# PSUM shared differently in a fused attention and mixture-of-experts kernel: three single banks for the maxima's scores, four for the exponentials', maxima read by head

## The chip, the cores and the metric

One core of one Trainium2 chip. The metric is device time in microseconds of one execution of the whole program. All arithmetic is in f32.

## What is computed

A transformer layer in "sandwich" form on x of shape (8, 1024, 256): layer norm, causal attention with 16 heads of 16, a second layer norm and a residual; then layer norm, a mixture of 8 experts (the best two of each token), layer norm and residual. The part that matters here is the attention:

```python
score = einsum('bhnd,bhmd->bhnm', q, k) * scale
score = where(causal, score, -inf)
attn = softmax(score, axis=-1)
out = einsum('bhnm,bhmd->bhnd', attn, v)
```

The experts come after it: `gu = flat @ gate_up[e] + bias`, a clipped gated product, `down`, and the two chosen results weighted and added.

## The kernel before

**Units and slots.** The attention works in 32 units: a unit is one batch entry (8) and a group of four heads (4 groups). For every unit two things are done, one unit apart. First the *maxima*: scores with the query on the partitions, of which only the row maxima are kept (`maxima_tiles`, L649). Then, one unit later, the *exponentials* of the same scores with the key on the partitions and the row maximum folded into the product (`values_tiles`, L758), so that ACT can take the exponential straight from PSUM (L796) and TensorE (PE) can multiply the result with the values (`weighted`, L810, matmuls at L825). So the main loop (L1151) in round u does the maxima of unit u and the exponentials of unit u - 1. Round 0 has maxima only, the last round exponentials only.

A unit has nine steps (`STEPS`, L635): two EDGE, three TWO, four WHOLE. In an EDGE step a 128x512 tile of scores ends on the diagonal; in a WHOLE step it lies under it; a TWO step packs two shorter tiles of one head into 512 columns. Every step is done for two pairs of heads, so a unit has 18 *slots*, and the attention 576, of which 558 have both halves. A slot (L1180 to L1232) issues in this order:

1. PE: four score matmuls, for the maxima's two heads (`sa`, L693) and for the exponentials' two heads (`sb`, L788). The four heads lie on different quarters of the partitions; a TWO step takes twice four, by part. Each matmul shows as two records in the trace.
2. ACT: the two exponentials (L796).
3. DVE, and ACT in TWO steps: the reading of `sa` (`reduce`, L698). WHOLE: one reduction of both heads (L709). EDGE: for each head an addition of the causal mask with a running maximum (L703, and the reading of its accumulator). TWO: a reduction of the blocks that need no mask for both heads (L718 or L724) and then a copy by ACT of the diagonal blocks of both heads into SBUF (L728), which POOL masks (L742) and DVE reduces (L747) later.
4. PE: one half of the weighted sums of an earlier step (L825), then background.

**Background.** Layer norms, projections, transposes, the output projection, routing: generators that yield pieces with a cost on each engine. `pump` (L1105) spends them against a credit that each slot earns (L1198 to L1204, with fixed numbers such as 1.22 us of DVE for a WHOLE slot). The order of PE, DVE, ACT and SP is the order of the source (`manual_schedule`, L1139), and POOL's is held by `in_order`.

**PSUM.** A bank is a tile of 128x512 f32, and the pools hold eight. During attention: `ps_a`, two buffers of two banks, a buffer for the maxima's scores of one slot (`sa`); `ps_v`, one bank for the weighted sums; `ps_b`, three single banks that rotate among the exponentials' scores (two a slot) and all of the background. In the last round pair 1 of the exponentials' scores takes a buffer of `ps_a` (L774). In the experts: `ps_gu`, four banks for the gate and up products of a quarter (L1305, read by DVE at L1317 and L1321), `ps_x`, one bank, and `ps_b`, three, for the down product (L1336) and what is left of the background. A bank is written again only when the reading of its last tile is over: PE waits at the first matmul of the new tile.

Of the kernel before, what the change touches and what calls it, by code (L numbers as in the profile page):

```python
# [11 lines left out]
F32 = mybir.dt.float32  # L12
AF = mybir.ActivationFunctionType
ALU = mybir.AluOpType
AX = mybir.AxisListType
PSUM = bass.MemoryType.PSUM

P = 128
# [40 lines left out]
def attn_moe_kernel(  # L59
# [15 lines left out]
    nc = tc.nc  # L75
    B, S, D = x.shape
# [3 lines left out]
    HG = P // HS  # L80
    NG = H // HG
# [3 lines left out]
    QC = 512  # L85
# [41 lines left out]
    cmask = const.tile([P, QC], F32, name="cmask")  # L127
    nc.gpsimd.memset(cmask, 0.0)
    nc.gpsimd.affine_select(
        out=cmask[:, QC - P :], in_=cmask[:, QC - P :], compare_op=ALU.is_ge, fill=NEG,  # L130
# [6 lines left out]
        out=lower, in_=lower, compare_op=ALU.is_gt, fill=0.0,  # L137
# [5 lines left out]
        out=upper, in_=upper, compare_op=ALU.is_gt, fill=0.0,  # L143
# [6 lines left out]
        out=before, in_=before, compare_op=ALU.is_gt, fill=0.0,  # L150
# [252 lines left out]
    tp = ctx.enter_context(tc.tile_pool(name="tables", bufs=1))  # L403
    ap2 = ctx.enter_context(tc.tile_pool(name="attn2", bufs=2))

    ps_b = ctx.enter_context(tc.tile_pool(name="ps_b", bufs=3, space=PSUM))

    with ExitStack() as attn:

# [1 line left out]
        ap1 = attn.enter_context(tc.tile_pool(name="attn1", bufs=1))  # L411
        ap3 = attn.enter_context(tc.tile_pool(name="attn3", bufs=2))
        ptp = attn.enter_context(tc.tile_pool(name="pt", bufs=3))
        ps_a = attn.enter_context(tc.tile_pool(name="ps_a", bufs=2, space=PSUM))
        ps_v = attn.enter_context(tc.tile_pool(name="ps_v", bufs=1, space=PSUM))


# [231 lines left out]
        def maxima_tiles(u):  # L649

            b, g = divmod(u, NG)
            qP, kP = qPs[u % NU], kPs[u % NU]
            mx = mxs[u % 2]
            edges = {}

            def rows(c):
                yield piece(dve=0.2)
                nm = ap2.tile([P, HG, n], F32, tag="nm", name=f"nm_{u}_{c}")
                nc.vector.tensor_reduce(nm, mx[:, :, ts(c, n), :], AX.X, ALU.max, negate=True)
                yield piece(pe=0.15, act=0.3, after=1)  # L660
                ps = ps_b.tile([HG * n, P], F32, tag="b", name=f"nmps_{u}_{c}")
                nc.tensor.transpose(ps, nm.rearrange("p h i -> p (h i)"), ident)
                nmT = ap2.tile([HG * n, P], F32, tag="nmT", name=f"nmT_{u}_{c}")
                nc.scalar.copy(nmT, ps)
                for hh in range(HG):
                    nc.sync.dma_start(
                        out=qP[hh * HS + DH : hh * HS + DH + 1, ts(c, QC)].rearrange(
                            "o (i q) -> o i q", q=P
                        ),
                        in_=nmT[ts(hh, n), :],  # L670
                    )

            left = [
                sum(c in {i // n for i, _, _ in tiles} for _, tiles, _ in STEPS)
                for c in range(NC)
            ]

            def of_two(k):

                (i, _, w), (i2, _, _) = STEPS[k][1]  # L680
                return slice(i, i2 + 1, i2 - i), w == P

            def pair_of_heads(k, pair):
                kind, tiles, _ = STEPS[k]
                ps = ps_a.tile([P, 2, QC], F32, tag="a", name=f"sa_{u}_{k}_{pair}")

                def scores(hh, part):
                    if part == len(tiles):
                        return
                    i, c, w = tiles[part]  # L690
                    at = sum(t[2] for t in tiles[:part])
                    r = ds((2 * pair + hh) * HS, HS)
                    nc.tensor.matmul(  # L693
                        ps[:, hh, ds(at, w)], lhsT=qP[r, ts(i, P)], rhs=kP[r, ds(c * QC, w)],
                        start=True, stop=True,
                    )

                def reduce():  # L698
                    heads = ts(pair, 2)
                    i, c, w = tiles[0]  # L700
                    if kind == EDGE:
                        for hh in range(2):
                            nc.vector.tensor_tensor_reduce(  # L703
                                out=ps[:, hh, :], in0=ps[:, hh, :], in1=cmask,
                                scale=1.0, scalar=NEG, op0=ALU.add, op1=ALU.max,
                                accum_out=mx[:, 2 * pair + hh, i, 0:1],
                            )
                    elif kind == WHOLE:
                        nc.vector.tensor_reduce(mx[:, heads, i, 2:3], ps, AX.X, ALU.max)  # L709
                    else:  # L710
                        both, short = of_two(k)
                        if k not in edges:
                            edges[k] = ap2.tile(
                                [P, HG, 2, P], F32, tag="edge", name=f"edge_{u}_{k}"
                            )
                        blocks = ps.rearrange("p h (b k) -> p h b k", k=P)
                        if short:
                            nc.vector.tensor_reduce(  # L718
                                mx[:, heads, tiles[1][0], 0:1], ps[:, :, P : 3 * P],
                                AX.X, ALU.max,  # L720
                            )
                            at = blocks[:, :, 0:4:3, :]
                        else:
                            nc.vector.tensor_reduce(  # L724
                                mx[:, heads, both, 0], blocks[:, :, 0:4:2, :], AX.X, ALU.max
                            )
                            at = blocks[:, :, 1:4:2, :]
                        nc.scalar.copy(edges[k][:, heads], at)  # L728

                return scores, reduce  # L730

            def counted_off(k):
                for c in {i // n for i, _, _ in STEPS[k][1]}:
                    left[c] -= 1
                    if not left[c]:
                        rows_of[u, c] = start(urgent, rows(c))

            def masked_edges(k):

                d = edges.pop(k)  # L740
                yield piece(pool=1.25)
                in_order(nc.gpsimd.affine_select(  # L742
                    out=d, in_=d, compare_op=ALU.is_ge, fill=NEG,
                    base=0, pattern=[[0, HG], [0, 2], [-1, P]], channel_multiplier=1,
                ))
                yield piece(dve=1.2, after=1)
                nc.vector.tensor_reduce(mx[:, :, of_two(k)[0], 1], d, AX.X, ALU.max)  # L747
                counted_off(k)

            def done(k):  # L750
                if k in edges:
                    start(urgent, masked_edges(k))
                else:
                    counted_off(k)

            return pair_of_heads, done

        def values_tiles(u):  # L758
# [11 lines left out]
            def pair_of_heads(k, pair):  # L770
                if k not in state:
                    state[k] = ptp.tile([P, HG, QC], F32, tag="pT", name=f"pT_{u}_{k}")
                pT = state[k]
                if u == B * NG - 1 and pair:  # L774
                    both = ps_a.tile([P, 2, QC], F32, tag="a", name=f"sb_{u}_{k}_{pair}")
                    banks = [both[:, hh, :] for hh in range(2)]
                else:
                    banks = [
                        ps_b.tile([P, QC], F32, tag="b", name=f"sb_{u}_{k}_{2 * pair + hh}")
                        for hh in range(2)  # L780
                    ]

                def scores(hh, part):
                    if part == len(STEPS[k][2]):
                        return
                    c, j, off, at = list(parts(k))[part]
                    r = ds((2 * pair + hh) * HS, HS)
                    nc.tensor.matmul(  # L788
                        banks[hh][:, ds(at, QC - off)], lhsT=kP[r, ts(j, P)],
                        rhs=qP[r, ds(c * QC + off, QC - off)],  # L790
                        start=True, stop=True,
                    )

                def exps():
                    for hh in range(2):
                        nc.scalar.activation(pT[:, 2 * pair + hh, :], banks[hh], AF.Exp)  # L796

                return scores, exps
# [446 lines left out]
    def pool(name, bufs, **where):  # L1245
        return ctx.enter_context(
            tc.tile_pool(name=name, bufs=bufs, reuse_waits="tile", **where)
        )
# [2 lines left out]
    m4 = pool("moe4", 4)  # L1251
    m2 = pool("moe2", 2)
    m1 = pool("moe1", 1)
    ps_gu = pool("ps_gu", 4, space=PSUM)
    ps_x = pool("ps_x", 1, space=PSUM)

    def load_tile(i):
# [298 lines left out]
```

## Time and profile before

| | |
|---|---|
| runs (3) | median 2213.28 us, 2211.36 to 2213.5 |
| the profiled execution | 2208.65 us, its span 2206.9 us |
| granted clock of TensorE | 0.992 of full speed |
| attention, both halves | from about 60 to 1372 us |
| last round, exponentials only | about 1374 to 1405 us |
| experts | from about 1407 us, the last layer norm ends the span |
| idle time of PE in the span | 64 us |
| DVE busy in 60 to 1400 us | 996 us |
| ACT busy in 60 to 1400 us | 839 us |

The profile is a hardware trace of one execution. PE stands for matmuls, PEld for the loading of their stationary operand, DVE, ACT, POOL and SP for the vector, scalar, GpSimd and sync engines. A line of a group has: line, engine, operation, what it writes and reads with shapes, how many; then busy us and mean ns of one; then the idle time of the engine just before them and what ended most of it. A line of the timeline has: start (us), length (us), engine, line, operation, tiles, shapes, how many merged; in brackets the idle time before and what ended it. A line of the stretches has for each engine its busy time and its count, then the granted clock, the share of DMA and GB/s.

### The profile page before, as it was taken

How to read it: one execution, taken by the hardware profiler on the slowest of the kernel's cores; microseconds unless marked ns; L12 is line 12 of the kernel's file. 1: busy time of each engine (PE TensorE's matmuls, PEld its weight loads, DVE VectorE, ACT ScalarE, POOL GpSimd, SP SyncE). 2: the span in 40 equal slices, each digit the busy share in tenths (PEclk: the TensorE clock that was granted, in tenths of full speed). 3: DMA queues.
4: the chain of work that ended last, by engine and by line, in shares of the span. 5: the costliest groups of instructions: out<-in, count | busy, mean ns of one | idle time of the engine just before them, and what ended most of it. 6: DMA issues, size and time to landing. Idle time of an engine off the chain costs nothing. (4 is left out here: it accounts for less than half of the span.)

```text
span 2206.9 us, 44890 instructions
## 1 busy us (share of the span) xinstructions
PE 2143.1 (97%) x16697; PEld 1330.8 (60%) x16697; DVE 1633.1 (74%) x3738; ACT 1086.1 (49%) x2169; POOL 1055.7 (48%) x1217
## 2 busy tenths in 40 slices
PE   7999999999999999999999999989999999999995
PEld 4444544544445445445444544678888888888885
DVE  4775777867767776786786787586667888888776
ACT  3666665665666666666666666431212322233222
POOL 3421652563573472482483364455444544445443
PEclk9999999999999999999999999999999999999998
DMA  4001102102101111111110111557657777877773
GB/s 107 17 10 34 29 12 59 41 21 59 33 29 38 50 33 26 45 50 22 50 50 13 39 43 38 173 198 252 220 203 260 261 269 259 273 260 243 261 268 123
DMA packets 138739, 246.70 MB, mean 112 GB/s; under 512 B 17472, under 2 KB 101592, under 8 KB 136600
## 3 DMA queue, kind: packets, MB, share of 16 engines
q1 hardware_dynamic: 124536, 208.22, 30.4%
q0 software_dynamic: 12768, 35.01, 4.2%
q8 instruction: 133, 2.18, 0.4%
q14 instruction: 86, 0.70, 0.1%
q10 hardware_dynamic: 1216, 0.58, 0.1%
HBM read 171.79 MB, written 55.23 MB: 103 GB/s over the span
## 5 line engine op out<-in xcount | busy, mean ns | idle before, releaser
L796 ACT ACTIVATE pT<-sb 128x512 f32<-128x512 f32 x1152 | 625.0, 595 | 409.4 <-PE sb L788 380.4
L788 PE MATMUL sb<-qP,kP 32*128 32x512 f32 (+3 forms) x3072 | 712.9, 524 | 2.9 <-DMA qP<-nmT 1.8
L693 PE MATMUL sa<-kP,qP 32*128 32x512 f32 (+3 forms) x3072 | 655.4, 525 | 3.4 <-DVE mx L703 1.4
L1308 PE MATMUL gu<-xsT,wg 128*128 128x256 f32 x2208 | 501.7, 379 | 0.8 <-ACT xsT L1290 0.7
L1308 PEld LDWEIGHTS gu<-xsT,wg 128*128 128x128 f32 x2208 | 418.4, 190 | 58.2 <-ACT xsT L1290 1.4
L805 POOL TENSOR_SCALAR_AFFINE_SELECT pT<-pT 128x512 f32<-128x512 f32 x256 | 159.6, 639 | 596.7 <-ACT pT L796 591.4
L709 DVE TENSOR_REDUCE mx<-sa 128x2 f32<-128x1024 f32 x256 | 311.5, 1218 | 112.3 <-PE sb L788 108.7
L1319 ACT ACTIVATE sig<-gate 128x256 f32<-128x256 f32 x276 | 114.9, 416 | 546.6 <-DVE gate L1317 545.3
L825 PE MATMUL av<-pT,vpad 128*32 128x256 f32 (+1 forms) x5120 | 345.6, 367 | 1.1 <-DVE avs L836 0.9
L693 PEld LDWEIGHTS sa<-kP,qP 32*128 32x128 f32 x3072 | 228.9, 185 | 189.0 <-issue 98.2
L1324 POOL TENSOR_TENSOR sig<-sig,gate 128x256 f32<-128x256 f32 x276 | 204.2, 742 | 268.8 <-ACT sig L1319 266.9
L788 PEld LDWEIGHTS sb<-qP,kP 32*128 32x128 f32 x3072 | 299.4, 184 | 41.4 <-ACT pT L796 7.2
L825 PEld LDWEIGHTS av<-pT,vpad 128*32 128x32 f32 x5120 | 116.4, 108 | 287.6 <-issue 210.2
L1339 PE MATMUL dn<-wd,act 128*128 128x256 f32 x1104 | 265.6, 381 | 7.8 <-DVE act L1329 7.4
L1317 DVE TENSOR_SCALAR gate<-gu,bs 128x256 f32<-128x256 f32 x276 | 131.8, 478 | 151.0 <-PE gu L1308 136.5
L1339 PEld LDWEIGHTS dn<-wd,act 128*128 128x128 f32 x1104 | 202.8, 190 | 39.4 <-DVE act L1329 15.4
L703 DVE CUSTOM_DVE_ANT_0 sa<-sa,cmask 128x512 f32<-128x512 f32 x256 | 178.0, 697 | 52.8 <-PE sb L788 28.3
L1349 POOL DMA_INDIRECT ytd<-ys,places x138 | 138.9, 1007 | 132.1 <-DVE ys L1345 104.6
L1046 POOL DMA_INDIRECT xsd<-xn,slots x128 | 126.8, 991 | 47.1 <-issue 29.6
L718 DVE TENSOR_REDUCE mx<-sa 128x2 f32<-128x512 f32 x128 | 88.1, 688 | 75.5 <-PE sb L788 49.7
L1329 DVE SCALAR_TENSOR_TENSOR act<-up,sig 128x256 f32<-128x256 f32 x276 | 128.3, 465 | 14.3 <-POOL sig L1324 14.3
L1321 DVE TENSOR_SCALAR up<-gu,bs 128x256 f32<-128x256 f32 x276 | 130.7, 473 | 0.0
(204 smaller groups left out, 2390.8 us busy)
## 6 DMA issues: line engine op xcount, KB each, us to landing
wg<-_L_ffn_gate_up_proj_dram SPq DMA_DIRECT2D x69, 1024.0 KB
wd<-in_L_ffn_down_proj_dram SPq DMA_DIRECT2D x69, 512.0 KB
xs<-xsd SPq DMA_DIRECT2D x65, 258.0 KB
yy<-ytd SPq DMA_DIRECT2D x15, 1024.0 KB
bs<-biasd SPq DMA_DIRECT2D x69, 132.0 KB
x<-in_L_attn_x_dram SPq DMA_DIRECT2D x16, 512.0 KB
x1d<-y SPq DMA_DIRECT2D x16, 512.0 KB
x<-x1d SPq DMA_DIRECT2D x16, 512.0 KB
```

Of the source, the lines that this page charges most:

```text
L693: nc.tensor.matmul(ps[:, hh, ds(at, w)], lhsT=qP[r, ts(i, P)], rhs=kP[r, ds(c * QC, w)], start=True, stop=True,)
L703: nc.vector.tensor_tensor_reduce(out=ps[:, hh, :], in0=ps[:, hh, :], in1=cmask, scale=1.0, scalar=NEG, op0=ALU.add, op1=ALU.max, accum_out ...
L709: nc.vector.tensor_reduce(mx[:, heads, i, 2:3], ps, AX.X, ALU.max)
L788: nc.tensor.matmul(banks[hh][:, ds(at, QC - off)], lhsT=kP[r, ts(j, P)], rhs=qP[r, ds(c * QC + off, QC - off)], start=True, stop=True,)
L796: nc.scalar.activation(pT[:, 2 * pair + hh, :], banks[hh], AF.Exp)
L805: in_order(nc.gpsimd.affine_select(out=d, in_=d, compare_op=ALU.is_ge, fill=0.0, base=0, pattern=[[0, HG], [1, P]], channel_multiplier=-1,))
L825: nc.tensor.matmul(av[ds(hh * HS, HS), ds(off + a - at, z - a)], lhsT=vp[:, j, ds((g * HG + hh) * VS, HS)], rhs=pT[:, hh, a:z],  start=c n ...
L1308: nc.tensor.matmul(ps[:, half, :], lhsT=wg[:, kt, ds(half * FF + f * P, P)], rhs=xT[:, kt, :], start=(kt == 0), stop=(kt == KT - 1),)
L1317: nc.vector.tensor_scalar(gt, ps[:, 0, :], bs[:, f : f + 1], LIMIT, ALU.add, ALU.min)
L1324: in_order(nc.gpsimd.tensor_tensor(sg, sg, gt, ALU.mult))
L1339: nc.tensor.matmul(ps[:, n, :], lhsT=act[:, f, ts(n, P)], rhs=wd[:, f, :], start=(f == 0), stop=(f == FT - 1),)
L1349: put = nc.gpsimd.indirect_dma_start(out=yt_dram[:, :], out_offset=bass.IndirectOffsetOnAxis(ap=places[:, i, n : n + 1], axis=0), in_=y[:, ...
```

## The change

The two pools of attention are cut differently: `ps_a` has three buffers of one bank, `ps_b` four. The maxima's scores are one tile for each head instead of one for a pair. `reduce` works by head: in WHOLE and TWO steps the reductions of a pair become two of half the length, and so does ACT's copy in TWO steps; EDGE already worked by head. In the last round pair 1 of the exponentials takes two single banks of `ps_a`. In the experts `ps_b` stays at four, and `ps_gu` goes from four to three. The costs that the planner uses are left as they were.

```diff
-    ps_b = ctx.enter_context(tc.tile_pool(name="ps_b", bufs=3, space=PSUM))
+    ps_b = ctx.enter_context(tc.tile_pool(name="ps_b", bufs=4, space=PSUM))
...
-        ps_a = attn.enter_context(tc.tile_pool(name="ps_a", bufs=2, space=PSUM))
+        ps_a = attn.enter_context(tc.tile_pool(name="ps_a", bufs=3, space=PSUM))
...
-                ps = ps_a.tile([P, 2, QC], F32, tag="a", name=f"sa_{u}_{k}_{pair}")
+                pss = [
+                    ps_a.tile([P, QC], F32, tag="a", name=f"sa_{u}_{k}_{2 * pair + hh}")
+                    for hh in range(2)
+                ]
...
-                        ps[:, hh, ds(at, w)], lhsT=qP[r, ts(i, P)], rhs=kP[r, ds(c * QC, w)],
+                        pss[hh][:, ds(at, w)], lhsT=qP[r, ts(i, P)], rhs=kP[r, ds(c * QC, w)],
...
-                    heads = ts(pair, 2)
+
                     i, c, w = tiles[0]
-                    if kind == EDGE:
-                        for hh in range(2):
+                    for hh, ps in enumerate(pss):
+                        h = 2 * pair + hh
+                        if kind == EDGE:
                             nc.vector.tensor_tensor_reduce(
-                                out=ps[:, hh, :], in0=ps[:, hh, :], in1=cmask,
+                                out=ps, in0=ps, in1=cmask,
                                 scale=1.0, scalar=NEG, op0=ALU.add, op1=ALU.max,
-                                accum_out=mx[:, 2 * pair + hh, i, 0:1],
+                                accum_out=mx[:, h, i, 0:1],
                             )
-                    elif kind == WHOLE:
-                        nc.vector.tensor_reduce(mx[:, heads, i, 2:3], ps, AX.X, ALU.max)
+                        elif kind == WHOLE:
+                            nc.vector.tensor_reduce(mx[:, h, i, 2:3], ps, AX.X, ALU.max)
...
+                            if short:
+                                nc.vector.tensor_reduce(
+                                    mx[:, h, tiles[1][0], 0:1], ps[:, P : 3 * P], AX.X, ALU.max
+                                )
+                                at = blocks[:, 0:4:3, :]
+                            else:
+                                nc.vector.tensor_reduce(
+                                    mx[:, h, both, 0], blocks[:, 0:4:2, :], AX.X, ALU.max
+                                )
+                                at = blocks[:, 1:4:2, :]
+                            nc.scalar.copy(edges[k][:, h], at)
...
-                if u == B * NG - 1 and pair:
-                    both = ps_a.tile([P, 2, QC], F32, tag="a", name=f"sb_{u}_{k}_{pair}")
-                    banks = [both[:, hh, :] for hh in range(2)]
-                else:
-                    banks = [
-                        ps_b.tile([P, QC], F32, tag="b", name=f"sb_{u}_{k}_{2 * pair + hh}")
-                        for hh in range(2)
-                    ]
+                at, tag = (ps_a, "a") if u == B * NG - 1 and pair else (ps_b, "b")
+                banks = [
+                    at.tile([P, QC], F32, tag=tag, name=f"sb_{u}_{k}_{2 * pair + hh}")
+                    for hh in range(2)
+                ]
...
-    ps_gu = pool("ps_gu", 4, space=PSUM)
+    ps_gu = pool("ps_gu", 3, space=PSUM)
```

## The prediction

> **What bounds the kernel now.** I read the page's shares first, then the groups, the stretches, and last the timeline of single slots.
>
> ```profile
> PE 2143.1 (97%) x16697; PEld 1330.8 (60%) x16697; DVE 1633.1 (74%) x3738; ACT 1086.1 (49%) x2169; POOL 1055.7 (48%) x1217
> ...
> L796 ACT ACTIVATE pT<-sb 128x512 f32<-128x512 f32 x1152 | 625.0, 595 | 409.4 <-PE sb L788 380.4
> L788 PE MATMUL sb<-qP,kP 32*128 32x512 f32 (+3 forms) x3072 | 712.9, 524 | 2.9 <-DMA qP<-nmT 1.8
> ...
> L709 DVE TENSOR_REDUCE mx<-sa 128x2 f32<-128x1024 f32 x256 | 311.5, 1218 | 112.3 <-PE sb L788 108.7
> ```
>
> ```profile
> 60.00:1400.00 1340.00, 1328.61 (x12752) 641.45 (x12749) 996.11 (x2144) 839.13 (x1621) 649.74 (x722) 1.00 0.14 36
> ```
>
> TensorE (PE) sets the pace; ACT and DVE mostly wait for it. The second fence is attention's steady stretch (PE, PEld, DVE, ACT, POOL busy): PE 1328.6 of 1340 us, DVE 996, ACT 839. That hides PE's waits, because a matmul's end is modelled. They show in starts. Call S the start of a slot's four score matmuls and R the start of what PE does next. With nothing waiting, R - S is 1.07 us (median 1.071 in the 369 one-tile slots). The tail, R to the next S, is fixed too: 0.569 us for one half of weighted sums alone, more with background.
>
> A WHOLE slot:
>
> ```profile
> 731.92 0.70 PE L788 MATMUL sb<-qP,kP 32*128 32x512 f32 x2
> ...
> 732.98 0.64 PE L825 MATMUL av<-pT,vpad 128*32 128x256 f32 x8
> 733.09 1.23 DVE L709 TENSOR_REDUCE mx<-sa 128x2 f32<-128x1024 f32 x1 [0.85 <-PE sb L788]
> 733.13 1.08 ACT L796 ACTIVATE pT<-sb 128x512 f32<-128x512 f32 x2 [0.99 <-PE sb L788]
> 733.55 0.19 PEld L693 LDWEIGHTS sa<-kP,qP 32*128 32x128 f32 x2 [0.41 <-issue]
> ...
> 733.56 0.91 PE L788 MATMUL sb<-qP,kP 32*128 32x512 f32 x2
> ```
>
> The row at 733.56 lasts 0.91 where 731.92 has 0.70: its second matmul waited 0.21 us for a ps_b bank, until the first exponential ended at 733.72 (release to PE 0.06). R comes at 734.83 instead of 734.62. Such waits, slot by slot over the 552 readable slots, are 69.2 us. 10.6 of them, in eight slots of the first interior TWO step, belong to the landing of nmT rows; 58.6 us are banks.
>
> A TWO slot:
>
> ```profile
> 703.24 0.64 PE L825 MATMUL av<-pT,vpad 128*32 128x256 f32 x8
> ...
> 703.41 0.68 DVE L724 TENSOR_REDUCE mx<-sa 128x4 f32<-128x512 f32 x1
> 703.45 1.09 ACT L796 ACTIVATE pT<-sb 128x512 f32<-128x512 f32 x2 [0.57 <-PE sb L788]
> ...
> 703.81 0.66 PE L856 MATMUL avt<-ident,avs 128*128 128x128 f32 x4
> 704.40 0.19 PEld L693 LDWEIGHTS sa<-kP,qP 32*128 32x128 f32 x2 [0.17 <-issue]
> ...
> 704.42 0.59 ACT L728 COPY edge<-sa 128x512 f32<-128x512 f32 x1
> ```
>
> R is 703.24, the next S 704.40. The edge copy stands behind both exponentials on ACT and starts at 704.42, after PE is already in the next slot. Today nobody waits: that slot has the other pair of banks.
>
> **The change, part by part.**
>
> *Fourth ps_b bank.* In a slot without background the bank of the second exponential's scores was last used two slots before, not one; with one background tile it is freed by the first exponential, at R + 0.72, while the tail is then 1.15. So the 58.6 us go. The last round, exponentials alone, has eight readable groups with 3.7 us of the same wait: take -3.
>
> *Three single ps_a banks.* Head 0 of a slot needs what head 1 had two slots before, head 1 what head 0 had one slot before. This is the new wait, at the head of PE's queue: behind it stand both sb matmuls, weighted sums and background, and for those wait ACT's exponentials and POOL's masks. It is paid in full unless the tail covers it. When head 0's bank comes free after R:
>
> - WHOLE: DVE starts at R + 0.105 (median of 193 starts from idle), a 512 reduction lasts 0.69 (L718's row, 688 ns for 512), release 0.06: 0.855.
> - EDGE: 0.105 + 0.75 (L703's 697 with its accumulator read, overlapped) + 0.06: 0.915.
> - TWO: exponentials start at R + 0.15, last 1.08, the copy overlaps them by 0.10, takes 0.38 (128x256 from PSUM: L447's rows, 383 ns), release 0.06: 1.57.
>
> Against the tails after these slots (slots, sum of what the tail leaves uncovered):
>
> | tail, us | TWO | EDGE | WHOLE |
> |---|---|---|---|
> | under 0.65 | 24: 24.0 | 37: 12.7 | 69: 19.7 |
> | 0.65-0.9 | 7: 5.1 | 23: 3.1 | 8: 0.9 |
> | 0.9-1.1 | 22: 12.5 | 13: 0 | 71: 0 |
> | 1.1-1.25 | 57: 23.3 | 27: 0 | 33: 0 |
> | 1.25-1.57 | 18: 4.4 | 14: 0 | 0 |
> | above | 55: 0 | 8: 0 | 66: 0 |
> | sum | 69.3 | 15.8 | 20.6 |
>
> 106 us if DVE always starts at once. It does not: with DVE and ACT where they really were in the trace, the sums are 66.4, 41.8 and 44.7, together 153 (short-tailed EDGE slots 0.86 us each, DVE being still at edge reductions of 1.2 us). The lower end could drop by 10: a wait of head 1 lets head 0's reduction start that much earlier relative to R, so in runs of WHOLE slots 0.29 alternates with nothing. A backlog also melts while PE waits, but not wholly, since DVE gets more to do. I take the middle, 130 (TWO 69, EDGE 30, WHOLE 31); ends 96 and 153.
>
> *Reductions by head.* 448 more DVE instructions (256 WHOLE, 192 TWO). Back to back, L709 takes 1138 ns from start to start and L718 601, so the fixed part is 64 ns: 29 us of DVE beside PE's work, inside the choice of 130. Here a rule speaks against the change: the Trainium skill's "Perfetto Trace Analysis", section Optimizing Scalar/DVE Operations, puts the overhead of each DVE operation on PSUM at about 125 ns of engine time and advises grouping where the engine is saturated. By that it is 56 us; the 27 more, spread over 558 slots, make DVE 0.05 us later in each, and in some 200 slots that wait for it add 10 us: +80 in all instead of +70. I use the row; DVE is not saturated in this stretch.
>
> *Edge copies by head.* 192 more on ACT: 192 x (2 x 0.38 - 0.59) = 33 us, beside PE (ACT 839 of 1340); their place on the path is in TWO's 1.57. If ACT had no slack it would cost those 33.
>
> *Nothing moved.* The planner's costs and the score order are unchanged; the built programs keep background in the same slots, and SP issues the same DMAs in the same order.
>
> *Round 0* (maxima alone) is held by DVE part of the time, 50 to 61 us, back-to-back L709: eight reductions split, 0.5 us; with EDGE and TWO take +1 (0 to 3).
>
> *Experts: ps_gu 3, ps_b 4.* A quarter's bank is read by two DVE operations, 478 and 473 ns, while the next two quarters fill; L1308 idles 0.8 us in 2208 matmuls. Zero, from -1 (dn's fourth bank) to +5 if DVE falls two quarters behind near 1406-1550, where background still runs.
>
> **Sum.** +130 - 58.6 - 3 + 1 = +69.4. On the profiled execution, 2208.65 (span 2206.9 and 1.75 around it): 2278. The median of the runs shown stands 4.6 above it: 2283.
>
> In the WHOLE slot above the exchange is small: head 1 would wait till 733.09 + 0.69 + 0.06 = 733.84, 0.28 late, where 0.21 was lost already. In the TWO slot it is not: copy 704.42 to 704.80, PE at 704.86, 0.46 us lost where nothing was.
>
> **Rivals.**
>
> *Backlog melts.* Waits 96: 96 - 58.6 - 2 = +35, 2249. For it: DVE has a quarter of the stretch free. Against: short-tailed EDGE slots are late by background DVE work, which stays. 20%.
>
> *DVE becomes the limit in EDGE and WHOLE.* Waits at 153, and 10 to 20 for the added instructions: some +106, 2319. For it: 0.86 us in short EDGE slots. If, too, the fourth bank did not release the exponentials' scores (the change not doing what it says), 58.6 more; the row at 733.56, ended by an exponential, speaks against that. 17%.
>
> *Faster.* The copy of head 0 gets ahead in TWO: ACT starts the exponentials early enough that the bank is free near R + 1.1, which the 1.1-1.25 tails cover (TWO about 25), and EDGE and WHOLE cost about 10. Then +35 - 60.6: 2188. It decides once all new waits sum below 60. Against: TWO alone gives 69, and its terms, exponentials first and then a copy, are measured rows. 6%.
>
> **How the numbers follow.** Likeliest, the middle: 57%, its own range 2262 to 2305. Range 2243 to 2325: it takes in most of the first rival and half of the second. About 0.2% is what a measurement here can tell from no change. Faster 6%; within it 2%, between the faster and the melting case; slower 92%.
>
> **What would show it.** In the new profile sb's waits on pT should vanish (R - S without the 0.21), while sa's second head waits: for the ACT edge copy after TWO slots, some 0.4 us each, 70 in all, and for DVE mx after EDGE and WHOLE, 60 in all. DVE busy should rise by about 30 us or less where spans overlap less, ACT by about 33, expert stretches unchanged. I am wrong if the waits after TWO are under 40 us, if sb still waits for exponentials, or if DVE's lag grows from slot to slot.

## The result, and the profile after

| | before | after |
|---|---|---|
| runs (4 each) | median 2212.32 us, 2206.56 to 2213.5 | median 2274.7 us, 2272.48 to 2278.0 |
| ratio to before | 1 | 1.0295 (95%: 1.0279 to 1.0311) |
| the profiled execution, its span | 2208.65, 2206.9 us | 2276.76, 2275.0 us |

The change costs 3%. The predicted 2283 us is 8.3 us above the median, and the range held it. The sum behind it was less right than its total: one term fell short by 21 us and others were too high by about as much.

The page of the profile after, its shares and groups:

```profile
PE 2204.6 (97%) x16697; PEld 1359.8 (60%) x16697; DVE 1655.0 (73%) x4186; ACT 1094.3 (48%) x2361; POOL 1058.2 (47%) x1217
...
L796 ACT ACTIVATE pT<-sb 128x512 f32<-128x512 f32 x1152 | 624.3, 595 | 488.6 <-PE sb L788 482.9
L696 PE MATMUL sa<-kP,qP 32*128 32x512 f32 (+3 forms) x3072 | 774.9, 529 | 20.1 <-ACT edge L731 13.4
L788 PE MATMUL sb<-qP,kP 32*128 32x512 f32 (+3 forms) x3072 | 653.5, 525 | 0.4 <-DMA qP<-nmT 0.4
...
L713 DVE TENSOR_REDUCE mx<-sa 128x1 f32<-128x512 f32 x512 | 328.0, 682 | 122.1 <-PE sb L788 103.4
```

Against the page of before: the busy time of sb's matmuls has fallen from 712.9 to 653.5 us, and sa's now has a releaser that was not there, ACT's edge copy (line 731, 728 before). A matmul's modelled end takes a wait of its own operands into its busy time, so most of the 59 us that left L788 must be bank waits. ACT's idle time before the exponentials rose by 79 us: ACT is not the engine that got longer, it waits for a PE that waits.

The stretch of attention, PE, PEld, DVE, ACT, POOL:

```profile
60.00:1400.00 1340.00, 1324.42 (x12096) 637.66 (x12094) 979.10 (x2459) 804.53 (x1716) 624.04 (x690) 0.99 0.13 34
```

PE is as "busy" as before (1328.6), but did 12096 matmul records in the same time where it did 12752, 5% fewer. The count tells what the busy time hides.

A WHOLE slot of after, with the short tail of 0.57 us:

```profile
602.21 0.64 PE L825 MATMUL av<-pT,vpad 128*32 128x256 f32 x8
602.30 1.29 DVE L713 TENSOR_REDUCE mx<-sa 128x1 f32<-128x512 f32 x2 [0.78 <-PE sb L788]
602.38 1.09 ACT L796 ACTIVATE pT<-sb 128x512 f32<-128x512 f32 x2 [0.99 <-PE sb L788]
...
602.78 0.95 PE L696 MATMUL sa<-kP,qP 32*128 32x512 f32 x2
603.05 0.19 PEld L788 LDWEIGHTS sb<-qP,kP 32*128 32x128 f32 x2
603.05 0.70 PE L788 MATMUL sb<-qP,kP 32*128 32x512 f32 x2
...
604.11 0.16 PEld L825 LDWEIGHTS av<-pT,vpad 128*32 128x32 f32 x8 [0.76 <-issue]
```

R is 602.21, the next S 602.78. sa's row lasts 0.95 where an unwaited one has 0.70: its second matmul waited for the bank that DVE's first reduction gave back near 603.0. sb follows at 603.05 with an unwaited 0.70. R - S is 604.11 - 602.78 = 1.33, so 0.26 us is lost; the prediction had 0.28 for this shape.

A TWO slot of after:

```profile
751.59 0.64 PE L825 MATMUL av<-pT,vpad 128*32 128x256 f32 x8
751.72 1.08 ACT L796 ACTIVATE pT<-sb 128x512 f32<-128x512 f32 x2 [0.98 <-PE sb L788]
...
752.41 1.40 PE L696 MATMUL sa<-kP,qP 32*128 32x512 f32 x3
...
752.69 0.66 ACT L731 COPY edge<-sa 128x256 f32<-128x256 f32 x2
...
753.12 0.18 PEld L696 LDWEIGHTS sa<-kP,qP 32*128 32x128 f32 x1 [0.42 <-ACT edge L731]
753.13 0.70 PE L788 MATMUL sb<-qP,kP 32*128 32x512 f32 x2
...
754.19 1.99 PE L600 MATMUL pjq<-xnT,wqT 128*128 128x512 f32 x4
```

R is 751.59, S 752.41. The copy of head 0 starts at 752.69, after both exponentials, and the load of sa's second head at 753.12 names it. Everything behind it on PE's queue is late with it: R - S is 754.19 - 752.41 = 1.78, 0.71 more than unwaited.

**Where the 68.1 us of the span are**, by the starts of PE's work in both traces:

| part | before to after, us | predicted |
|---|---|---|
| round 0, to the first sb (59.7, now 73.4) | +13.7 | +1 |
| round 1 (18 slots) | +8.5 | in the next row |
| slots from 36 on: score groups | +60.1 | +71.4 (130 - 58.6) |
| the same slots: tails | -11.6 | 0 |
| last round, exponentials alone | -2.7 | -3 |
| experts | +0.1 | 0 |

### The profile page after: what moved, and what is told of

It reads as the page before. It is cut to its first block, busy times and chain, and to the rows that moved or that the text cites. A ratio compares the mean times of both kernels' runs of the same rounds, so it can differ in the third digit from the quotient of the medians.

```text
span 2275.0 us, 45369 instructions
## 1 busy us (share of the span) xinstructions
PE 2204.6 (97%) x16697; PEld 1359.8 (60%) x16697; DVE 1655.0 (73%) x4186; ACT 1094.3 (48%) x2361; POOL 1058.2 (47%) x1217
## 5 line engine op out<-in xcount | busy, mean ns | idle before, releaser
L696 PE MATMUL sa<-kP,qP 32*128 32x512 f32 (+3 forms) x3072 | 774.9, 529 | 20.1 <-ACT edge L731 13.4
L788 PE MATMUL sb<-qP,kP 32*128 32x512 f32 (+3 forms) x3072 | 653.5, 525 | 0.4 <-DMA qP<-nmT 0.4
L696 PEld LDWEIGHTS sa<-kP,qP 32*128 32x128 f32 x3072 | 300.0, 186 | 258.2 <-issue 87.7
L713 DVE TENSOR_REDUCE mx<-sa 128x1 f32<-128x512 f32 x512 | 328.0, 682 | 122.1 <-PE sb L788 103.4
L788 PEld LDWEIGHTS sb<-qP,kP 32*128 32x128 f32 x3072 | 251.1, 185 | 19.9 <-issue 1.7
L707 DVE CUSTOM_DVE_ANT_0 sa<-sa,cmask 128x512 f32<-128x512 f32 x256 | 172.6, 711 | 62.8 <-PE sa L696 25.8
L722 DVE TENSOR_REDUCE mx<-sa 128x1 f32<-128x256 f32 x256 | 96.8, 419 | 101.8 <-PE sb L788 54.1
```

The source lines that it names most:

```text
L696: nc.tensor.matmul(pss[hh][:, ds(at, w)], lhsT=qP[r, ts(i, P)], rhs=kP[r, ds(c * QC, w)], start=True, stop=True,)
L707: nc.vector.tensor_tensor_reduce(out=ps, in0=ps, in1=cmask, scale=1.0, scalar=NEG, op0=ALU.add, op1=ALU.max, accum_out=mx[:, h, i, 0:1],)
L713: nc.vector.tensor_reduce(mx[:, h, i, 2:3], ps, AX.X, ALU.max)
L788: nc.tensor.matmul(banks[hh][:, ds(at, QC - off)], lhsT=kP[r, ts(j, P)], rhs=qP[r, ds(c * QC + off, QC - off)], start=True, stop=True,)
```

## The experiments

Ratios are against the kernel before on the same chip; "slot waits" are R - S - 1.07 us summed over the slots after 100 us, as in the prediction: 67.5 before (sb 64.3) and 129.3 after (sa 126.4, sb 2.9). After was not timed again beside the experiments: before stood at 2212.32 us in its measurement and at 2205.5 to 2209.1 in these. A distance to after is therefore good to some us only, and where it matters the one by ratios stands beside the one by medians.

**Is it the splitting or the banks?** Maxima by head, but with the banks shared as before:

```diff
-        ps_a = attn.enter_context(tc.tile_pool(name="ps_a", bufs=3, space=PSUM))
+        ps_a = attn.enter_context(tc.tile_pool(name="ps_a", bufs=4, space=PSUM))
```

(ps_b 3 and ps_gu 4 again.)

> The changed kernel with its reductions and edge copies by head, but with four single banks for the maxima's scores (as many as before), three for ps_b and four for ps_gu: only the splitting is left. Theory (the loss is head 0's bank coming free too late, one slot back): sa has its old distance of two slots, so within 0.5% of before, 2201 to 2224 us; DVE about 25 us busier, ACT up to 33. Rival (the added DVE and ACT instructions are what costs): about the changed kernel's 2275.

2206.55 us, ratio 0.9997 (0.9986 to 1.0008); slot waits 70.1, sb's as before. The 448 reductions and 192 copies more (DVE busy +13.1 us) cost nothing that shows. One bank moved from the maxima to the exponentials costs the rest.

**Does the fourth ps_b bank give anything?** The change with it taken away again, so that one bank lies unused:

```diff
-    ps_b = ctx.enter_context(tc.tile_pool(name="ps_b", bufs=4, space=PSUM))
+    ps_b = ctx.enter_context(tc.tile_pool(name="ps_b", bufs=3, space=PSUM))
```

> The changed kernel with ps_b back at three banks (one bank unused): the loss without the gain. Theory: the waits of sa stay (about 125 us in the steady stretch) and those of sb for exponentials come back where they are not covered by the wait of sa in the same slot: 2300 to 2340 us, 25 to 65 above the changed kernel. Rival (the fourth bank gave nothing, since exponentials limit sb by their own speed): the changed kernel's 2275 within 0.3%.

2300.15 us, 1.042 (1.0393 to 1.0447): 25 us above after (28 by ratios). sb's waits are back at 34.7, while sa's fell to 108.8: while PE waits for the one, the other comes free. So the bank is worth less than the waits that it removes, and the fourth ps_a bank, which is missing, costs more than it gives. Both halves of the exchange are real.

**Is it the copy's place behind the exponentials?** In TWO steps ACT does exponential, copy, exponential, copy:

```diff
...
-                        for _, use in reversed(heads):
-                            use()
+                        if first and second and STEPS[k][0] == TWO:
+                            for hh in range(2):
+                                for _, use in reversed(heads):
+                                    use((hh,))
+                        else:
+                            for _, use in reversed(heads):
+                                use()
```

(`reduce` and the exponentials also take the heads that they work on.)

> The changed kernel with ACT's order in TWO slots turned from exponential, exponential, copy, copy into exponential, copy, exponential, copy. Theory: head 0's bank then comes free near R + 1.09 us instead of 1.57, so the 76 us of waits after TWO slots fall to about 17, the rest stays: 2210 to 2230 us. Rival (it is the copy's length and DVE's reduction that hold the bank, not the place behind the exponentials): over 2260.

2257.72 us, 1.023 (1.0204 to 1.0256): 17 us better than after (14 by ratios, 22 between the profiled executions), not the 45 or more expected. Its waits, in the view of waits (engine, what waited, for whom; us, times, longest):

```profile
PEld sa L696 <- DVE mx L714: 51.7, 134, 1.6
PEld sa L696 <- ACT edge L732: 29.8, 74, 1.5
PEld sa L696 <- DVE mx L708: 28.1, 47, 2.1
```

The same three rows of after:

```profile
PEld sa L696 <- DVE mx L713: 43.6, 112, 1.8
PEld sa L696 <- ACT edge L731: 43.2, 96, 1.5
PEld sa L696 <- DVE mx L707: 17.6, 41, 1.7
```

ACT's row shrinks and both of DVE's grow. Slot by slot: after TWO slots the waits fall from 76 to 41.7 (sa 31.2, sb 10.5), after EDGE they rise from 22.4 to 32.4, after WHOLE from 28.0 to 36.9. The place behind the exponentials was indeed what held the bank: the first copy ends at R + 1.06 in the median of the TWO slots, where after had 1.52. Two things were left out of the expected gain. In 34 of 183 TWO slots the copy still ends after R + 1.15; in 28 of these it stood idle for DVE's reduction of the same scores, and the second exponential stood behind it:

```profile
648.80 0.60 ACT L797 ACTIVATE pT<-sb 128x512 f32<-128x512 f32 x1 [0.84 <-PE sb L789]
650.04 0.37 ACT L732 COPY edge<-sa 128x256 f32<-128x256 f32 x1 [0.65 <-DVE mx L728]
650.31 0.60 ACT L797 ACTIVATE pT<-sb 128x512 f32<-128x512 f32 x1
```

Behind these 34 slots lie some 19 of the 41.7 us. And the waits share one slack: a PE that waits less in TWO steps meets a DVE that has had less time. Readings that stand just behind an edge reduction cost 16 us in 26 slots of after and 34 us in 44 slots here. Of the 22 us between the two profiled executions, 7.7 lie before slot 36 and not in the slots at all: round 0 is the same in both kernels, but the granted clock of 20 to 100 us was higher in this run (0.91 and 0.87 over two stretches of 40 us, where after had 0.83 and 0.70).

**Round 0.** Pair 1 of the maxima takes ps_b banks there, where no exponentials are in progress:

```diff
+                of, tag = (ps_b, "b") if u == 0 and pair else (ps_a, "a")
                 pss = [
-                    ps_a.tile([P, QC], F32, tag="a", name=f"sa_{u}_{k}_{2 * pair + hh}")
+                    of.tile([P, QC], F32, tag=tag, name=f"sa_{u}_{k}_{2 * pair + hh}")
```

> The changed kernel, except that in round 0 (maxima alone) the scores of pair 1 take ps_b's banks, which the exponentials do not yet use. In the changed kernel the first 36 slots with both halves start 22 us later than before; 13 us of that is there when round 1 begins. Theory: this is the same wait, sa for the read of the slot just before, in front of the projections: 2255 to 2265 us (10 to 20 less than the changed kernel), and the granted clock of the first 100 us goes back up with it. Rival (the lower granted clock of the first 100 us is chance of the run and makes the 22 us): 2270 to 2278.

2262.04 us, 1.0251 (1.0225 to 1.0277): 12.7 us below after (10 by ratios, 15.5 by spans). The first sb comes at 57.2 us, before the 59.7 of the kernel before; the later slots have the same differences to before as after has (+60.0, -11.6). So the loss of round 0 is the three banks' and can be had back alone.

**Both.** e3 and e4 together.

> The changed kernel with ACT's order in TWO slots turned (exponential, copy, exponential, copy) and pair 1 of round 0 in ps_b's banks, the two cures together. Each alone took about 13 to 22 us off the changed kernel. Theory: they lie in different stretches and add up: 2235 to 2248 us. Rival (both only spare the low granted clock of the first 100 us): no less than the better of the two, 2255.

2245.77 us, 1.0169 (1.0145 to 1.0193). The two gains add: 28.9 us below after in medians, where the single ones sum to 29.7 (28 and 24 by ratios).

**The exponentials' scores first.** On top of that, sb's matmuls ahead of sa's on PE, so that ACT starts before R:

```diff
-                            for scores, _ in heads:
+                            for scores, _ in reversed(heads):
```

> The kernel with both cures, and PE's order within a slot turned as well: first the scores of the exponentials, then those of the maxima. Theory: the wait of sa no longer holds up sb, so ACT begins earlier against PE, head 0's bank comes free earlier after TWO slots, and the waits there (about 42 us with the first cure) halve; those after EDGE and WHOLE are DVE's and stay: 10 to 25 us less than with both cures, 2215 to 2235. Rival (sb's place in the queue is of no account, PE pays the wait all the same): the same time as both cures within 0.2%.

2232.6 us, 1.0115 (1.0091 to 1.0139). A TWO slot of it:

```profile
626.42 0.60 ACT L798 ACTIVATE pT<-sb 128x512 f32<-128x512 f32 x1
...
626.65 0.64 PE L827 MATMUL av<-pT,vpad 128*32 128x256 f32 x8
...
627.01 0.37 ACT L733 COPY edge<-sa 128x256 f32<-128x256 f32 x1
...
627.22 0.48 PE L790 MATMUL sb<-qP,kP 32*128 32x256 f32 x2
...
627.23 0.68 PE L697 MATMUL sa<-kP,qP 32*128 32x256 f32 x2
```

ACT starts 0.23 us ahead of R, the copy ends at R + 0.73, where after's first copy ended near R + 1.5. sa still loses 0.2 us (0.68 for 0.48). Waits after TWO are 31.7 (sa 20.6, sb 11.1), after EDGE 35.0, after WHOLE 35.9: most of what is left belongs to DVE. This is the best form of the change that I have, and it is slower than before.

**What is DVE's lateness worth?** The 96 reductions of the masked edges done twice (the second gives the same result), some 107 us more of DVE, in both kernels:

```diff
-                nc.vector.tensor_reduce(mx[:, :, of_two(k)[0], 1], d, AX.X, ALU.max)
+                for _ in range(2):
+                    nc.vector.tensor_reduce(mx[:, :, of_two(k)[0], 1], d, AX.X, ALU.max)
```

> The changed kernel with every edge reduction on DVE (128x1024 out of SBUF, 96 of them) done twice, the second time with the same result: 96 x 1.13 = 108 us more on DVE and nothing else. Theory: with sa at a distance of one slot DVE's lateness is paid by PE, above all in the slots after EDGE and WHOLE: 20 to 60 us on top of the changed kernel. Rival (DVE has room, the waits after EDGE and WHOLE are only the fixed 0.855 and 0.915 us): under 8 us more.

> The kernel before with the same 96 edge reductions done twice: 108 us more on DVE. Theory: with two slots of distance DVE's lateness is covered: under 8 us more than before. Rival (DVE is near its limit in this stretch whatever the banks): as much more as the changed kernel loses by it, 20 to 60 us.

In after 2363.86 us, 1.0704 (1.0679 to 1.0729); in before 2262.75, 1.0245 (1.0221 to 1.027). Both cost more than expected, and the second misses outright: I had taken the two-slot distance for cover, and it is not. By spans, a microsecond of DVE costs 86.8/108.2 = 0.80 us in after and 58.8/105.8 = 0.56 in before. In before the scores give 20.9 of it and the tails 31.3. Part of the tails is sa itself, at two slots: PE stood idle there for 12.7 us just before sa's first matmul (1.9 in before) and for 8.8 us before the transposes of the finished maxima (3.9); the rest I did not take apart. The bank distance makes DVE dearer; it is not what makes it matter.

**Can DVE be relieved?** The copies of the finished sums (64, 0.69 us each) go from DVE to ACT, in before, in after and in e6:

```diff
-                        nc.vector.tensor_copy(avs, av)
+                        nc.scalar.copy(avs, av)
```

> The kernel before with the 64 copies of the weighted sums out of PSUM (128x512, 0.69 us each) on ACT instead of DVE: 44 us of DVE work gone, 38 us on ACT; the order of everything else unchanged. Doubling the edge reductions cost this kernel 57 us for 108 us of DVE work. Theory (DVE's lateness is partly paid even at two slots of distance): 5 to 20 us less than before. Rival (that cost came from the edge reductions' own place, late maxima, and DVE has room): within 0.2% of before, or slower, since the copies now stand in front of exponentials on ACT.

> The changed kernel with the same 64 copies on ACT. Theory: after EDGE and WHOLE slots PE waits for a late DVE, so these waits (50 us) shrink by 15 to 30; after TWO slots ACT is later by a copy in some: 2245 to 2265 us. Rival (the waits after EDGE and WHOLE are the fixed length of one reading): no less than the changed kernel, or more.

> The best of the changed kernels so far (copy between the exponentials, round 0 in ps_b, exponentials' scores first, 2232.6 us) with the same 64 copies on ACT. Theory: what is left there is mostly DVE's lateness (70 us after EDGE and WHOLE), so it gains more than the changed kernel does: 2200 to 2220 us, which would be level with before. Rival: 2230 or more.

All three theories miss, and each result lies on its rival's side. Before becomes 2223.88, 1.0073 (1.0057 to 1.0089); after 2277.5, 1.0323 (1.0301 to 1.0345), which can't be told from after's 1.0295; e6 becomes 2244.28, 1.0164 (1.014 to 1.0189). e10's waits:

```profile
PEld sa L696 <- DVE mx L713: 43.5, 113, 1.6
PEld sa L696 <- ACT edge L731: 42.7, 93, 1.5
PEld sa L696 <- DVE mx L707: 17.9, 41, 2.0
```

44 us of DVE are gone and the rows are those of after. These copies are not what stands before the readings. In the 70 slots of after in which PE waits for a reading that DVE began late, DVE's operation just before it is an edge reduction in 26, the layer norms' statistics in 21, a small operation of the routing in the rest, and such a copy in none. On ACT they stand beside the exponentials: in before the waits after TWO slots grew by 9.7 us.

**Shorter pieces before the readings.** In before, the edge reductions in two halves that the planner may put into different slots:

```diff
-                yield piece(dve=1.2, after=1)
-                nc.vector.tensor_reduce(mx[:, :, of_two(k)[0], 1], d, AX.X, ALU.max)
+                for pair in range(2):
+                    yield piece(dve=0.6, after=1)
+                    h = ts(pair, 2)
+                    nc.vector.tensor_reduce(mx[:, h, of_two(k)[0], 1], d[:, h], AX.X, ALU.max)
```

> The kernel before with every edge reduction (1.2 us of DVE, in front of a reading of scores) cut into two halves of two heads, which the planner puts into different slots. Theory (in both kernels a reading of scores that stands behind an edge reduction is late, and doubling that reduction cost the kernel before 57 us): half the length ahead of a reading, 5 to 20 us less than before, so a version faster than both kernels: 2186 to 2201 us. Rival (the doubling cost its 57 us through the bulk of DVE work, or through what the planner then finds no room for): within 0.3% of before, or slower by the 96 more instructions.

2216.48 us, 1.0046 (1.0031 to 1.0061), the rival's side. Its profile splits the result: from the first gate matmul to the end 809.0 us instead of 797.9, while that matmul comes 3.3 us earlier (1405.7). Slot waits are 69.4. So smaller pieces shorten no wait of these slots. Only some 3 of before's 67.5 us are sa's, so there was little of that kind to shorten; in after, where 26 slots pay 16 us behind an edge reduction, the halves were not tried. And the planner, whose costs changed with them, left more background to the experts (3711 matmul records from the first gate matmul on, 3678 in before). Their timeline, where the routing ends:

```profile
1542.05 0.81 PE L343 MATMUL tabps<-two,ones 128*128 128x142 f32 x2 [2.44 <-DVE two L340]
1542.66 5.82 PE L1310 MATMUL gu<-xsT,wg 128*128 128x256 f32 x16
```

PE's idle time after the first gate matmul is 4.4 us more than before (20.4 against 16.0), and the 16 gate matmuls behind the last wait take 5.82 us instead of the 3.62 of their like, 2.2 more (the granted clock was 0.50 from 1540.3 to 1547.1 us). The other 4.5 are about what attention got rid of (3.3) and 1 that I have not placed. No kernel tried beats before.

## Why the prediction was right, by its own steps

**The new waits, +130** (TWO 69, EDGE 30, WHOLE 31): 126.4, as 76.0, 22.4 and 28.0. The terms and their owners held. The price of a TWO slot was right: the one shown has its release at R + 1.53 (753.12), assumed was 1.57. There are more of them, 136 that wait where the table had 128, because the tails got shorter: in after's trace 137 tails after TWO slots are under 1.57 us, and the table's sum over them is 76.4. For EDGE and WHOLE the measured 50 lies between "DVE always on time" (36) and "DVE as late as in the trace of before" (87), somewhat below the 61 that was chosen. Some 38 of these microseconds lie in 70 slots where DVE began its reading over 0.15 us after R; in 26 of these, with 16 us, the edge reduction (L750, 1.2 us) stands just before it. e3 shows why the middle: a wait in one slot gives DVE time in the next.

**The fourth ps_b bank, -58.6 and 10.6 that stay:** the term that was too small. sb's waits fell by 61.4, so the landing of the nmT rows, meant to stay, mostly vanished behind sa's waits. And the tails gave 11.6 that the sum had at nothing. I had fixed the tails, though background tiles take ps_b banks too. With three ps_b banks (e2) the tails give 6.2, so about half of it is the bank; the other half would be operands that are ready sooner because PE is late, which is argued, not shown.

**Round 0, +1 (0 to 3): wrong.** It measured +13.7, and 8.5 more in round 1. The other runs with the same round 0 (e2, e3, e10) lost 10.7 to 14.0 us by the first sb and 14.5 to 22.6 by slot 36. I priced the added instructions and left out the distance: with pairs of two banks DVE has a slot and its tail for a reading, with three singles the second head of a slot waits for the reading of the slot just before, behind projections that the schedule puts between them. The timeline of after in round 0:

```profile
33.77 0.76 DVE L722 TENSOR_REDUCE mx<-sa 128x1 f32<-128x256 f32 x2 [2.23 <-PE sa L696]
34.23 0.70 ACT L731 COPY edge<-sa 128x256 f32<-128x256 f32 x2 [0.93 <-DVE mx L722]
34.65 0.72 PEld L696 LDWEIGHTS sa<-kP,qP 32*128 32x128 f32 x6 [1.53 <-ACT edge L731]
34.66 1.13 PE L696 MATMUL sa<-kP,qP 32*128 32x256 f32 x6 [0.91 <-ACT edge L731]
...
35.71 3.68 PE L586 MATMUL vps<-wvT,xnT 128*128 128x256 f32 x8
```

PE stands 0.91 us, and then eight matmuls that take 1.99 us elsewhere take 3.68: the granted clock fell. The windows from 20 to 100 us, before and then after (the granted clock third from the end):

```profile
20.00:60.00 40.00, 36.43 (x168) 17.32 (x169) 22.31 (x37) 10.74 (x22) 3.70 (x4) 0.95 0.42 98
60.00:100.00 40.00, 38.69 (x363) 18.27 (x359) 31.23 (x62) 25.52 (x50) 19.74 (x21) 0.92 0.04 8
```

```profile
20.00:60.00 40.00, 36.41 (x134) 18.08 (x133) 15.12 (x37) 10.39 (x26) 3.64 (x4) 0.83 0.35 86
60.00:100.00 40.00, 35.60 (x194) 16.53 (x191) 23.01 (x53) 12.29 (x28) 10.82 (x13) 0.70 0.08 15
```

They give the lost clock as (1 - clock) x length: 5.2 us before, 18.8 after. By this estimate 13.6 of the 22.2 us are clock and 8.6 are left for the waits themselves. e4 took away the round's part of both at once, so the split between them rests on this sum and not on a run of its own. e4 recovers 17.0 of the 22.2 by slot 36 (+5.2 there).

**Last round -3:** -2.7. **Experts 0:** +0.1; the ps_gu bank that was given up costs nothing there.

**DVE +29, off the path:** +21.9 (1633.1 to 1655.0; e1, with the same instructions, +13.1), and e1 shows it off the path. The rule weighed against it, about 125 ns of overhead for each operation, would be 56 us; nothing here comes near. **ACT +33:** +8.2. Two copies of 128x256 in a row take 0.66 us together (752.69), not 2 x 0.38, against 0.59 for the one they replace: they overlap. The first one's own 0.37, which the path sees, was right.

**The rivals.** The backlog does not melt to 96 us, nor does DVE hold the waits at 153. The faster one needed all new waits under 60: even e6, which moves the exponentials ahead of R as that rival asked, has 91.5 us of sa's left (35.0, 35.9 and 20.6).

**The sum:** on spans it was +69.4 against +68.1, with +21 missed early, and against it 11 too few in the tails, 3 in the banks, 4 too many in the waits and 3 more of waits that sa already had. Errors of opposite sign met, so it is luck that the two sums lie within 1.3 us of each other. The medians differ by 62.4 only, since before's profiled execution lay 3.7 us under its median and after's 2.1 above.

## What to carry to other kernels

When banks are moved between two users, count for each the slots from the reading of a bank to its next writing, and lay the reader's real start and end against the tail: here the step from two slots to one cost some 123 us (sa's waits were 3.2 us before and 126.4 after), and a spare bank on the other side gave back 61, and about half of the 12 in the tails. Do it for the start of the kernel too, where the other user does not run yet and its banks lie idle. Waits of one in-order engine share their slack: taking away 34 us in one place gave 15 in all, since 19 came back in another.

## What the runs showed of the hardware that was not expected

At the start, lost clock went with short stands of PE. The windows of after (PE's busy time and count first, the granted clock third from the end):

```profile
39.30:42.70 3.40, 2.50 (x14) 1.28 (x14) 1.60 (x5) 1.29 (x3) 0.99 (x1) 1.00 0.82 185
42.70:46.10 3.40, 3.40 (x11) 2.23 (x13) 1.66 (x3) 0.08 (x1) 0.11 (x1) 0.50 0.11 30
46.10:49.50 3.40, 2.55 (x14) 1.01 (x15) 2.06 (x7) 0.58 (x2) 0.00 (x0) 1.00 0.00 0
49.50:52.90 3.40, 3.40 (x11) 1.26 (x11) 0.16 (x1) 1.20 (x4) 0.00 (x0) 0.50 0.01 4
...
73.40:97.30 23.90, 21.82 (x121) 11.16 (x119) 12.70 (x33) 9.89 (x23) 9.74 (x11) 0.50 0.01 2
97.30:120.00 22.70, 22.34 (x225) 9.94 (x221) 17.96 (x39) 14.27 (x29) 10.09 (x11) 1.00 0.01 2
```

In these rows a window in which PE is busy 2.5 of 3.4 us is followed by one at half clock, which, being slow, is full, and the clock comes back. Then a half-clock stretch of 23.9 us follows; from 97 us on the clock stays at 1.00, with single waits of 0.5 to 1 us still there. What ends it is open.

The Trainium skill's "TensorE: Matmul & The Clock Gate", section "What's actually happening", gives the two states, half and full, and a window of about 3.4 us, and these rows agree (3.4 us, 0.50 and 1.00). The page's rule against idle gaps of more than about 3.4 us (section "HAM oscillation — how this bites in real kernels") does not cover this: the gaps in round 0 are 0.77 to 0.92 us. Nearer is its section "A second HAM failure mode: psum-queue depth-cycling": small idle times between groups that cycle through banks can make the clock swing. Some of the runs fit that: with four ps_a banks in e1 the clock was 1.00 through 20 to 100 us, in e2, with round 0 as in after, 0.83 and 0.70 again. Others show that a stand alone does not decide it. e3 has the same round 0, and with stands of the same length it kept the full clock for 23.9 us:

```profile
47.30:71.20 23.90, 19.84 (x70) 7.10 (x71) 14.32 (x26) 3.84 (x9) 1.10 (x1) 1.00 0.26 66
```

In e1 single stands of 1.76 and 1.12 us (at 41 and 75 us) cost no clock, while in before half-clock stretches of 3.4 and 6.8 us came after stands of 1.96 and 1.31 us. e4, without the waits of round 0, has

```profile
20.00:60.00 40.00, 34.93 (x178) 17.62 (x177) 24.40 (x55) 13.48 (x32) 3.82 (x4) 1.00 0.43 99
60.00:100.00 40.00, 36.74 (x309) 17.35 (x307) 26.01 (x64) 20.91 (x46) 17.43 (x20) 0.79 0.01 2
```

The first stretch is free of it; the second, where three banks work beside the exponentials, is not, but there before too has 0.92. So more stands went with more lost clock in these runs, and which of them costs some is open. A kernel's own time moves with it: of before's executions on one chip, one took 2204.09 us at a granted clock of 0.994 and another 2214.38 us at 0.989.
